# Repacking the pair products of a three-layer CIN kernel: six passes of 128 rows and a shared half pass, operands and weights gathered by row lists

## The chip, the cores and the metric

The kernel runs on one core of one Trainium2 chip, in float32. The metric is the device time of one execution in microseconds. All times quoted are medians of fast runs unless said otherwise. On one core most executions of a kernel agree within about 1%.

## The reference, cut to what matters

```python
B, F, E = (1024, 39, 64)       # batch of x, fields, embedding
HID = [64, 64, 64]

def _cin_layer(Xk, X0, W, b):
    O = W.shape[0]
    Hk, Fdim = (Xk.shape[1], X0.shape[1])
    Wr = W.reshape(O, Hk, Fdim)
    return jnp.einsum('bhe,bfe,ohf->boe', Xk, X0, Wr) + b[None, :, None]

X0 = Xk = sparse_embedding
outs = []
for W, b in ((W0, b0), (W1, b1), (W2, b2)):
    Xk = _cin_layer(Xk, X0, W, b)
    outs.append(Xk.sum(axis=-1))
y = jnp.concatenate(outs, axis=-1) @ fc_w.T + fc_b
```

Both kernels use that only sums over E of the later layers reach the output. The first layer's products x_b * x_a are symmetric, so 39 * 40 / 2 = 780 distinct products a column are enough. A set of weights with 128 columns per chunk of products gives the first layer's 64 outputs and 64 further rows, into which W1, W2 and fc_w were folded beforehand. What remains is one multiplication of the two halves, a sum over E and a small final matmul. "Preparation" below is the folding of the weights and the first fetching of operands.

## The kernel before

The 65536 columns (1024 x 64) are taken in 32 blocks of 2048. The 39 fields lie doubled in DRAM, and four "rolled" copies of 117 = 3 x 39 rows are read from there. A chunk is the elementwise product of two rolls. Six pairs of rolls give 702 products; a seventh chunk, from a roll and a tile q, holds the other 78 and the 39 single fields.

```python
NG = 3
K = NG * F                                   # 117 rows
PAIRS = ((0, 1), (0, 2), (1, 2), (0, 3), (1, 3), (2, 3))
NCHUNK = len(PAIRS) + 1                      # 7

def store(n):
    xd[n] = xds.tile([FW, BLK], F32, name="xd", tag="xd")
    nc.sync.dma_start(xd[n][0:F], xs[n])
    nc.sync.dma_start(xd[n][F:FW], xs[n])

def roll(n):
    r[n] = [rolls.tile([K, BLK], F32, name=f"r{i}", tag=f"r{i}") for i in range(4)]
    for i in range(4):
        nc.sync.dma_start(r[n][i], rows(xd[n], BASE[i], [(1, F), (STEP[i], NG)], BLK))
    qt = q[n % 2]
    nc.sync.dma_start(qt[0:K:NG], xd[n][LAST : LAST + F])
    nc.sync.dma_start(qt[1:K:NG], xd[n][0:F])
# ... preparation: fold W2 (pv, vrow, v2), fold W1 (pt, part), write both doubled to DRAM
#     (wide), gather wa and wb back from there ...
def multiply(n, c, p):
    if c == 0:
        po[n] = [psum.tile([128, SUB], F32, name="po", tag="po") for _ in range(BLK // SUB)]
    for m in range(BLK // MM):
        nc.tensor.matmul(po[n][m // 2][:, bass.ts(m % 2, MM)], wa[:, c, :],
                         p[:, bass.ts(m, MM)], start=(c == 0), stop=(c == NCHUNK - 1))

AHEAD = 4
steps = [(n, c) for n in range(NBLK) for c in range(NCHUNK)]
p = {s: product(*s) for s in steps[:AHEAD]}
for at, (n, c) in enumerate(steps):
    # ... at c == 0: roll(n + 1), store(n + 2), load(n + 3) ...
    if n == 0:
        nc.vector.tensor_tensor(wa[:, c], wa[:, c], wb[:, c], ALU.add)
    multiply(n, c, p.pop((n, c)))
    # ... at c == 0: finish(n - 1), fields(n) ...
    if at + AHEAD < len(steps):
        p[steps[at + AHEAD]] = product(*steps[at + AHEAD])
```

## Time and profile before

| | before |
|---|---|
| time, median of the runs | 862.5 us (861.8 to 863.8) |
| span of the profiled execution (its own time 858.7) | 856.9 us |
| PE busy / DVE busy | 93% / 77% |
| PE without a pause | 97 to 846 us |
| one chunk of 4 matmuls in steady state | 3.442 us |
| lost before PE is full, counted in whole chunks | 76.5 us |
| tail after the last matmul | 9.4 us |

In profiles PE is TensorE, PEld its weight loads, DVE VectorE, ACT ScalarE, POOL GpSimd and SP SyncE; a "q" behind an engine marks the DMAs that it issues.

The profile is read from the outside in. The page says which engine is full and when. The chain of waits says what the end hangs on, and the stretches give each engine's load in the steady part. The timeline then shows what the start waits for. The f32 matmul appears as two records, so one 4-matmul chunk is 8 records. A record's duration includes its latency, so neighbours overlap; the cost of a chunk is read from the spacing, not from the mean.

### The profile page before, as it was taken

What the parts mean: (1) busy time and instruction counts of PE and PEld (TensorE: products, weight loads), DVE (VectorE), ACT (ScalarE), POOL (GpSimd) and SP (SyncE); (2) the same over time, 40 slices, a digit from 0 to 9 for tenths busy, and PEclk for the clock granted to TensorE, in tenths of its full rate; (3) what the DMA queues carried; (4) which work ended last, traced back from release to release, by engine and by line L of the source; (5) the groups of instructions that cost most, each with busy time, mean ns of one, the idle gap of its engine ahead of it and who ended that gap; (6) DMA issues with size and microseconds to landing.
All of it is one profiled execution on the core that took longest, in us unless ns stands there. A gap on an engine that the chain in (4) does not pass through costs nothing.

```text
span 856.9 us, 5040 instructions
## 1 busy us (share of the span) xinstructions
PE 794.1 (93%) x1828; PEld 346.0 (40%) x1828; DVE 664.1 (77%) x372; ACT 140.9 (16%) x133; POOL 44.0 (5%) x54
## 2 busy tenths in 40 slices
PE   1446799999999999999999999999999999999996
PEld 0112344444444444444444444444444444444442
DVE  0333488888888888888888888888888888888883
ACT  0010121122221111122222111122222111112221
POOL 4200000000000000000000000000000000000000
PEclk9998999999999999999999999999999999999998
DMA  6957645767666666665766666755776666565500
GB/s 187 255 142 241 241 177 197 230 210 218 254 240 234 213 233 218 221 215 211 248 242 251 196 237 195 244 215 216 237 242 251 215 225 232 193 210 204 187 0 1
DMA packets 32177, 179.41 MB, mean 209 GB/s; under 512 B 8487, under 2 KB 8686, under 8 KB 11901
## 3 DMA queue, kind: packets, MB, share of 16 engines
q1 hardware_dynamic: 25003, 164.63, 54.9%
q0 software_dynamic: 4080, 11.11, 5.8%
q10 hardware_dynamic: 3070, 3.35, 1.3%
q8 instruction: 14, 0.23, 0.1%
q14 instruction: 10, 0.08, 0.0%
HBM read 156.98 MB, written 23.61 MB: 211 GB/s over the span
## 4 chain that ended last, share of the span: by engine, by line
PE 89%; DMA 7%; issue 1%; DVE 1%; ACTq 1%; SPq 0%; ACT 0%; DVEq 0%
PE po L239 89%; DMA wide<-part 2%; DMA xs<-in_x 2%; DMA r<-xd 1%; DMA v<-vrow 1%; DMA xd<-xs 1%; ACTq L197 1%; DMA wa<-wide 0%; DVE g L262 0%; DVE sums L266 0%; PE pt L186 0%; PE py L295 0%; SPq L200 0%; DVE wa L282 0%; DMA q<-xd 0%
## 5 line engine op out<-in xcount | busy, mean ns | idle before, releaser
L239 PE MATMUL po<-p,wa 117*128 117x512 f32 x1792 | 778.8, 597 | 34.6 <-DVE wa L282 34.6
L232 DVE TENSOR_TENSOR p<-r,r 117x2048 f32<-117x2048 f32 x192 | 436.8, 2289 | 142.9 <-PE po L239 132.3
L239 PEld LDWEIGHTS po<-p,wa 117*128 117x128 f32 x1792 | 342.9, 192 | 469.9 <-issue 422.4
L258 ACT ACTIVATE x<-po,b0s 64x1024 f32<-64x1024 f32 x64 | 71.1, 1112 | 495.7 <-PE po L239 495.7
L251 ACT COPY g<-xs 39x1024 f32<-39x1024 f32 x64 | 66.7, 1043 | 156.4 <-DVE sums L266 156.4
L262 DVE SCALAR_TENSOR_TENSOR g<-po,fc,x 64x1024 f32<-64x1024 f32 x64 | 81.1, 1268 | 9.8 <-ACT x L258 9.8
L266 DVE TENSOR_REDUCE sums<-g 103x16 f32<-103x1024 f32 x64 | 78.1, 1220 | 2.2
L232 DVE TENSOR_TENSOR p<-r,q 117x2048 f32<-117x2048 f32 x32 | 73.1, 2284 | 3.8 <-issue 3.8
L98 POOL DMA_DIRECT2D xs<-in_x x31 | 30.1, 975 | 680.3 <-DMA xd<-xs 397.6
L186 PE MATMUL pt<-w1s,v 64*80 64x512 f32 (+1 forms) x10 | 9.5, 1109 | 13.7 <-DVE v L178 13.7
L222 ACT ACT_TABLE_LOAD x1 | 1.3, 1283 | 57.0 <-DMA wb<-wide 57.0
L186 PEld LDWEIGHTS pt<-w1s,v 64*80 64x80 f32 x10 | 2.2, 228 | 20.4 <-DVE v L178 14.7
L178 DVE COPY v<-v 64x39 f32<-64x39 f32 x1 | 0.2, 176 | 12.9 <-DMA v<-vrow 12.9
L169 PE MATMUL pv<-w2s,fc 64*32 64x312 f32 x16 | 2.5, 724 | 7.9 <-DVE fc L159 7.3
L188 DVE COPY part<-pt 80x512 f32<-80x512 f32 (+1 forms) x5 | 3.4, 673 | 6.8 <-PE pt L186 6.8
L295 PE MATMUL py<-sums,wfin 103*1 103x512 f32 x4 | 2.9, 814 | 3.7 <-DVE sums L266 3.7
L159 DVE COPY fc<-fc 64x32 f32<-64x32 f32 x1 | 0.2, 173 | 6.0 <-DMA fc<-in_fc_w 6.0
L197 POOL DMA_DIRECT2D wa<-wide x6 | 4.1, 686 | 9.5 <-DMA wide<-in_w0t 9.0
L197 POOL DMA_DIRECT2D wb<-wide x6 | 4.3, 716 | 2.2 <-DMA wb<-wide 2.2
L169 PEld LDWEIGHTS pv<-w2s,fc 64*32 64x32 f32 x16 | 0.4, 137 | 9.0 <-DVE fc L159 7.3
L152 POOL MEMSET q<- 117x2048 f32 x2 | 3.6, 1843 | 0.0
L176 DVE COPY vrow<-pv 128x312 f32<-128x312 f32 x2 | 1.0, 482 | 2.7 <-PE pv L169 2.7
(22 smaller groups left out, 9.1 us busy)
## 6 DMA issues: line engine op xcount, KB each, us to landing
r<-xd SPq DMA_DIRECT2D x128, 936.0 KB
xd<-xs SPq DMA_DIRECT2D x64, 312.0 KB
q<-xd SPq DMA_DIRECT2D x64, 312.0 KB
xs<-in_x POOLq DMA_DIRECT2D x31, 312.0 KB, 5.2
wide<-part ACTq DMA_DIRECT2D x8, 160.0 KB
wide<-in_w0t POOLq DMA_DIRECT2D x2, 380.2 KB, 9.7
wide<-in_w0t ACTq DMA_DIRECT2D x2, 380.2 KB
w2s<-in_w SPq DMA_DIRECT2D x1, 624.0 KB
```

Source lines behind the costliest of these rows:

```text
L98: engine.dma_start(xs[n].rearrange("p (b e) -> p b e", e=E), xv[:, n * BB : (n + 1) * BB, :])
L152: nc.gpsimd.memset(qt, 1.0)
L169: nc.tensor.matmul(pv[32 * t : 32 * t + 32, half, 0:n8], fc2, w2s[:, g * n8 : (g + 1) * n8], start=True, stop=True,)
L186: nc.tensor.matmul(pt[0:FX, :n], v2, w1v[:, f0:f1, :], start=True, stop=True)
L188: nc.vector.tensor_copy(part[:, :n], pt[0:FX, :n])
L197: engine.dma_start(dst[:, cols], rows(table, first, steps, H))
L232: nc.vector.tensor_tensor(p, a, b, ALU.mult)
L239: nc.tensor.matmul(po[n][m // 2][:, bass.ts(m % 2, MM)], wa[:, c, :], p[:, bass.ts(m, MM)], start=(c == 0), stop=(c == NCHUNK - 1),)
L251: nc.scalar.copy(gt[H : H + F], xs[n][:, bass.ts(h, SUB)])
L258: nc.scalar.activation(t, po[n][h][H:128, :], AF.Identity, bias=b0s[H:128])
L262: nc.vector.scalar_tensor_tensor(gt[0:H], po[n][h][0:H, :], fc[:, 0:1], x1[h], ALU.add, ALU.mult)
L266: nc.vector.tensor_reduce(sums[:, b_at : b_at + SB], gt.rearrange("p (b e) -> p b e", e=E), AX.X, ALU.add)
```

## The change

The intent was to waste fewer rows of TensorE. Six chunks of 128 rows hold 768 of the 780 products, and what is left over (12 products and 39 single fields) fits into 64 rows, so that two blocks share one pass, each in its own half of the array's rows. The odd row sets can't be described by strides, so operands and weights are fetched by lists of row numbers from tables in DRAM, with indirect DMAs from GpSimd ("gathers"). In the code, r holds the four gathered tiles of a block, u and v are the two factors of a pair's shared half pass, and wa and wb are two gathered sets of weights that VectorE adds once (the "weight add"). The preparation was rebuilt around those tables and its order changed. The core of the diff:

```diff
-NCHUNK = len(PAIRS) + 1
+PAIRS = ((0, 1), (0, 2), (0, 3), (1, 2), (2, 3), (1, 3))
+NPAIR = len(PAIRS)
+NCHUNK = NPAIR + 1
 ...
+    def gather_rows(dst, n, k):
+        table = xd[n // 2 % NTAB][: FT if k < 4 else 2 * FT]
+        nc.gpsimd.indirect_dma_start(
+            dst, None, table, bass.IndirectOffsetOnAxis(ap=lists[:, k : k + 1], axis=0)
+        )
 ...   (lists and wlists: about 60 tiny VectorE instructions from an iota)
+    def weights(c):
+        for k, w in enumerate((wa, wb)):
+            nc.gpsimd.indirect_dma_start(
+                w[:, c], None, table[:], bass.IndirectOffsetOnAxis(ap=wlists[:, k, c : c + 1], axis=0)
+            )
+    weights(0)
+    roll(0, (3,))
+    weights(1)
+    weights(2)
+    roll_half(0)
+    weights(3)
+    roll(1, (0, 1))
+    weights(4)
+    roll(1, (2, 3))
+    weights(5)
+    weights(6)
 ...   (multiply, when c == NPAIR)
+            for h in range(2):
+                w = slice(h * HR, (h + 1) * HR)
+                nc.tensor.matmul(
+                    po[n + h][m // 2][:, at],
+                    wa[w, c, :],
+                    p[w, bass.ts(m, MM)],
+                    start=(h == 1),
+                    stop=(h == 0),
+                )
 ...   (first block)
-        if n == 0:
-            nc.vector.tensor_tensor(wa[:, c], wa[:, c], wb[:, c], ALU.add)
+        if at == 0:
+            for k in range(3):
+                nc.vector.tensor_tensor(wa[:, k], wa[:, k], wb[:, k], ALU.add)
+                if k < 2:
+                    p[steps[2 + k]] = product(*steps[2 + k])
+        elif n == 0 and c + 2 < NCHUNK:
+            nc.vector.tensor_tensor(wa[:, c + 2], wa[:, c + 2], wb[:, c + 2], ALU.add)
```

The small loads of biases moved behind the table's writes, and the last small matmuls (last_weights, with wfin's memset) behind the last block.

## The prediction

> **What bounds the kernel now.** I read the page first (busy shares, slices, costly groups), then the chain in order of time, then the stretches, then the start instruction by instruction. The page, sections 1, 2, 3 and 5:
>
> ```profile
> PE 794.1 (93%) x1828; PEld 346.0 (40%) x1828; DVE 664.1 (77%) x372; ACT 140.9 (16%) x133; POOL 44.0 (5%) x54
> PE   1446799999999999999999999999999999999996
> ...
> q1 hardware_dynamic: 25003, 164.63, 54.9%
> ...
> L239 PE MATMUL po<-p,wa 117*128 117x512 f32 x1792 | 778.8, 597 | 34.6 <-DVE wa L282 34.6
> L232 DVE TENSOR_TENSOR p<-r,r 117x2048 f32<-117x2048 f32 x192 | 436.8, 2289 | 142.9 <-PE po L239 132.3
> ```
>
> PE is full from the sixth slice to the last but one, VectorE (DVE) at eight tenths waits for PE (132.3 us of it), and the only idle time of the main matmul group, 34.6 us, lies at the start. Next the chain in order of time, then the stretches (PE, PEld, DVE, ACT, POOL busy; clock; DMA share; GB/s):
>
> ```profile
> 97.15 748.60 PE po L239 x1740
> 845.83 1.12 ACT x L258
> ```
> ```profile
> 97.00:846.00 749.00, 748.85 (x1741) 331.54 (x1742) 629.99 (x339) 133.78 (x125) 26.11 (x27) 1.00 0.62 213
> ```
>
> From 97 to 846 us PE never pauses, at full clock, while DMA is at 0.62. So a matmul removed there is time gained. A chunk is 8 records (each of the 4 matmuls of 512 columns is two records in f32), so one chunk costs 748.60/(1740/8) = 3.442 us. The kernel has 32 blocks of 7 chunks: 224 x 3.442 = 771.0 us. PE's last chunk ends at about 847.5 us (the tail's second activation starts at 847.55), so 847.5 - 771.0 = **76.5 us are lost at the start**, and 856.9 - 847.5 = 9.4 us are tail. The start, by the timeline:
>
> ```profile
> 15.25 3.04 ACTq L177 DMA_DIRECT2D v<-vrow  x2
> 23.89 0.18 DVE L178 COPY v<-v 64x39 f32<-64x39 f32 x1 [12.87 <-DMA v<-vrow]
> 27.03 15.02 ACTq L190 DMA_DIRECT2D wide<-part  x10
> 46.26 0.87 ACTq L197 DMA_DIRECT2D wa<-wide  x1
> 53.03 6.84 PE L239 MATMUL po<-p,wa 117*128 117x512 f32 x8 [19.04 <-DVE wa L282]
> 59.91 2.29 DVE L232 TENSOR_TENSOR p<-r,r 117x2048 f32<-117x2048 f32 x1 [6.93 <-PE po L239]
> 62.12 0.28 DVE L282 TENSOR_TENSOR wa<-wa,wb 117x128 f32<-117x128 f32 x1
> 62.46 5.40 PE L239 MATMUL po<-p,wa 117*128 117x512 f32 x8 [2.59 <-DVE wa L282]
> ```
>
> Weights pass through DRAM twice (vrow, then part and wide), so the first chunk waits until 53.03. Then block 0 goes in lockstep: a product waits for PE to free its buffer, the weight add stands behind it on DVE, and PE waits for the add: 19.0 us once, then six times about 2.6. Its restarts are slow too (6.84, 5.40 us against 3.442).
>
> **What the Trainium skill says.**
> (1) "TensorE: Matmul & The Clock Gate", Part 3, has matmuls in different row tiles run together, and four K=32 row tiles measured 3.07 times faster. The trace has no row tiles, but it has column tiles in f32:
>
> ```profile
> 7.34 1.27 PE L169 MATMUL pv<-w2s,fc 64*32 64x312 f32 x8 [7.34 <-DVE fc L159]
> ```
>
> Eight records that span 724 ns each (the page) are over in 1.27 us, against 8 x 724 = 5.8 us end to end: they overlap nearly fully. It agrees for columns.
> (2) "TensorEngine Tiling (Array Packing)", Key Properties: changing the mode drains TensorE. No view here prices it.
> (3) "DMA: Bandwidth & Descriptors", the section on why a semaphore goes up by 16: the number of engines is the largest divisor up to 16 of both slowest dims. 117 partitions from 39 rows would give 13 of 16; 128 rows 16. The page's DMA share is a mean over engines and neither confirms nor refutes it.
> (4) "SBUF — State Buffer", SBUF: two separate sides: GpSimd and DVE share a port pair, and descriptors of GpSimd's DMAs can be held up by certain DVE instructions. The trace cannot show it yet: only 5.8% of engine time is on that queue.
>
> **The change part by part.**
> *Chunks.* Before, a block pair takes 14 chunks. After, it takes 12 full ones and one pass that holds both blocks' remainder in rows 0-63 and 64-127: 8 matmuls of 64 rows, in two row tiles and into different banks. The record count stays at 12 x 8 + 16 = 112 a pair, 1792 in all, so only overlap gains. With full overlap the pass costs one chunk, 3.44, plus my estimate of 0.5 us for two drains and a staggered start: 3.94. Pair: 12 x 3.442 + 3.94 = 45.24 against 48.19. Sixteen pairs: 723.8 against 771.0, **-47.2 us**. More rows in a matmul cost nothing: its time goes by the 512 columns.
> *DVE.* 13 products a pair instead of 14: 13 x 2.29 + 4 x (1.27 + 1.22) = 39.7 of 45.2 us, 88%; before 42.0 of 48.2. It stays beside PE.
> *DMA.* A block now gathers 4 MiB for r and half of 2 x 1 MiB for u and v, 5.24 MB, and loads 0.32 MB DRAM to DRAM: 5.56 MB per 22.6 us = 246 GB/s. Before it was 4 x 0.958 + 5 x 0.319 = 5.43 MB per 24.1 us = 225. Per engine: 164.63 MB/(0.549 x 16 x 856.9 us) = 21.9 GB/s, so 16 engines could do some 350. Estimated share about 0.75: hidden if the software queue is as good. r is double, so the next block's gathers have well over a block (about 30 us) between the last read of the old tile and the first product. Five indirect gathers a block at 1 to 2 us of GpSimd each (plain DMAs there take 0.6 to 1.0 us) are at most 10 of 22.6 us.
> *Start.* Estimates from the same operations before. Row lists: some 40 tiny DVE instructions of about 0.1 us, 4 to 5 us, while w2 and x load; lists at 7, x in the table at 8 to 9, three r gathers landed by 20. pv needs one round instead of two: vrow at 11, v2 by 17 (its DMA took 7.8 us before, under traffic). Five pt matmuls now sit two by two in column tiles and their copies are shared with ScalarE: last part at 24.5 instead of 34. Five table writes instead of ten, on two queues: table at 32 instead of 45. Two gathers of 128 rows give chunk 0 its weights: first matmul at about 38 instead of 53. Chunk 0 cold, to 44.5. Then the add is two chunks ahead, so the six waits of 2.6 us and the slow restarts go; but the later weights stand in GpSimd's queue behind 1 MiB gathers (r3, u, v, r of block 1: 7 MiB at 250 to 340 GB/s), so chunks 3 to 5 arrive late by some 7 to 10 us together. I put the end of block 0's seven chunks at 69.6 us: lost 69.6 - 7 x 3.442 = **45.5 against 76.5, -31 us**.
> *Tail.* last_weights moves behind the last block and wfin's memset behind the last reduce on DVE, so both py matmuls wait for it: about +1 us on 9.4.
> Sum: 45.5 + 723.8 + 10.4 = 779.7 us of span. Runs are 862.5 - 856.9 = 5.6 us above the span: 785.3, rounded to **786 us**.
>
> **The rivals.**
> (a) *The row tiles don't overlap.* The pass costs 16 records x 0.43 = 6.9 us, PE gains nothing in the steady part, and only the start counts: 16 x (6.9 - 3.9) = 48 more, 834 us. For it: no row-tiled f32 record in this trace. Against it: the overlap of pv. 13%.
> (b) *The software queue becomes the bound.* If gathers by row lists move below 246 GB/s, say 200, a block takes 5.56/0.2 = 27.8 us and the kernel 900; at 230, 24.2 us and some 840. For it: that queue is barely used now, DVE could hold up descriptors, and its 256-byte writes ran at 11.11 MB/(0.058 x 16 x 856.9) = 14 GB/s an engine. Against it: rows of 8 KB and all 16 engines. 8%.
> (c) *The start gains little*, because one gather queue serializes weights and operands: lost 60 instead of 45.5, 800 us. 20%. Or the traffic is faster than I think: 38, 778 us.
> (d) *DVE becomes the bound*: 39.7 us a pair leaves 5.5; it needs waits of over 0.4 us a product. 4%.
>
> **Range and chances.** The middle is the sum. Down: start at 36 and drains free give about 768. Up: start at 60 plus a half overlap of the pass (+24) gives 824. Rival (a) alone is at 834 and still over 2% faster (845 is the line); only (b) or (d) can reach it. Faster 0.95, within 2% 0.03, slower 0.02.
>
> **What would show it.** In the profile after: a form of 64 x 512 matmuls, 256 records, the pass taking about 3.9 us between full chunks (6.9 if (a)); full chunks still 3.44; PE without waits after block 0 (waits of DVE for r gathers every block if (b)); DVE near 88%; DMA near 0.75 and 246 GB/s; the first main matmul near 38 us and the end of block 0 near 70; a tail of 10 to 11 us. I am wrong if row tiles take turns, if gathers land over 30 us after they are asked for, or if table writes of 256 bytes are far slower than the old ones of 2 KB.

## The result, and the profile after

The kernel after takes 777.5 us (777.1 to 780.9, 4 runs) against 862.3 us for the kernel before in the same rounds. The ratio is 0.902, with a 95% interval of 0.8995 to 0.905. A ratio here is the mean time of one kernel's fast runs over that of the other's fast runs of the same rounds, so it is not quite the ratio of the medians. The profiled execution (777.1 us) has a span of 775.1 us.

The page of the kernel after: busy shares, PE in 40 slices, the gather queue, and the groups that answer to those shown of before:

```profile
PE 735.6 (95%) x1820; PEld 316.8 (41%) x1820; DVE 633.2 (82%) x409; ACT 142.2 (18%) x136; POOL 279.2 (36%) x185
...
PE   3279999999999999999999999999999999999996
...
q0 software_dynamic: 23840, 169.46, 56.0%
...
L341 PE MATMUL po<-p,wa 128*128 128x512 f32 x1536 | 667.8, 596 | 19.3 <-DVE wa L409 15.1
L324 DVE TENSOR_TENSOR p<-r 128x2048 f32<-128x2048 f32 x192 | 435.9, 2291 | 96.9 <-PE po L341 68.3
...
L117 POOL DMA_INDIRECT r<-xd,lists x128 | 211.3, 1651 | 410.5 <-DVE p L324 384.0
...
L352 PE MATMUL po<-p,wa 64*128 64x512 f32 x256 | 59.3, 602 | 0.0
```

PE is now full from the fourth slice. The bulk of the bytes moved from the hardware queue to GpSimd's software queue (q0). There is a new group of 256 matmul records of 64 rows, and its 59.3 us of busy time for records that would take 256 x 0.43 = 110 us in a row says at once that they overlap.

The chain in order of time (start, length, what) gives the price of a pass, and one stretch of a block pair in the steady part gives the load of each engine, in the order of columns told in the prediction:

```profile
63.71 3.63 PE po L352 x16
67.34 41.40 PE po L341 x96
```
```profile
350.00:395.30 45.30, 45.30 (x114) 19.81 (x113) 39.12 (x22) 8.62 (x8) 16.38 (x11) 1.00 0.65 246
```

A half pass costs 3.63 us and twelve full chunks 41.40 us, so a pair costs 45.03 us where it cost 14 x 3.442 = 48.19 us. PE still has no pause, DVE works 39.12 of 45.30 us (86%), and DMA moves 246 GB/s at a share of 0.65.

The start, by the timeline (start, length, engine, line, what, and what ended the idle time before):

```profile
7.75 1.32 SPq L246 DMA_DIRECT2D v<-vrow  x2
...
13.87 5.61 PE L273 MATMUL pt<-w1s,v 64*40 64x512 f32 x10 [6.70 <-DMA v<-vrow]
...
27.41 0.95 POOL L298 DMA_INDIRECT wa<-table,wlists  x1 [11.24 <-DMA bias<-in_b]
...
33.32 5.45 PE L341 MATMUL po<-p,wa 128*128 128x512 f32 x8 [13.84 <-DVE wa L409]
...
53.90 0.29 DVE L413 TENSOR_TENSOR wa<-wa,wb 128x128 f32<-128x128 f32 x1 [5.33 <-DMA wb<-table,wlists]
...
54.24 5.24 PE L341 MATMUL po<-p,wa 128*128 128x512 f32 x8 [3.68 <-DVE wa L413]
...
63.64 3.70 PE L352 MATMUL po<-p,wa 64*128 64x512 f32 x16
```

The first main matmul starts at 33.32 us where it started at 53.03. Later weights are late, though: at 53.90 DVE has waited 5.33 us for the weights of chunk 4, PE therefore 3.68 us, and its restart is slow (5.24 us; from 54.0 to 57.4 us the granted clock is 0.50). Block 0 ends at 67.3 us.

Put together in spans, with PE's last chunk ending at 847.5 us before and 763.7 us after:

| part | before | after | gain |
|---|---|---|---|
| sixteen block pairs | 771.0 | 16 x 45.03 = 720.5 | 50.5 |
| lost at the start (end of PE less the line above) | 76.5 | 43.2 | 33.3 |
| tail (span less end of PE) | 9.4 | 11.4 | -2.0 |
| span | 856.9 | 775.1 | 81.8 |

### The profile page after: what moved, and what is told of

Read it like the earlier page. It is cut to its first block, busy times and chain, and to the rows that moved or that the text cites. A ratio compares the mean times of both kernels' runs of the same rounds, so it can differ in the third digit from the quotient of the medians.

```text
span 775.1 us, 4926 instructions
## 1 busy us (share of the span) xinstructions
PE 735.6 (95%) x1820; PEld 316.8 (41%) x1820; DVE 633.2 (82%) x409; ACT 142.2 (18%) x136; POOL 279.2 (36%) x185
## 3 DMA queue, kind: packets, MB, share of 16 engines
q0 software_dynamic: 23840, 169.46, 56.0%
## 4 chain that ended last, share of the span: by engine, by line
PE 92%; DMA 3%; POOL 2%; DVE 2%; issue 1%; ACT 0%; SPq 0%; POOLq 0%; DVEq 0%; ACTq 0%
PE po L341 83%; PE po L352 8%; DMA r<-xd,lists 1%; DMA table<-part 1%; POOL wa L298 1%; DMA v<-vrow 1%; DMA wb<-table,wlists 1%; POOL r L117 1%; PE pt L273 1%; PE py L427 0%; POOL wb L298 0%; DVE g L376 0%; DVE sums L380 0%; DMA bias<-in_b 0%; DVE fields_of L196 0%
## 5 line engine op out<-in xcount | busy, mean ns | idle before, releaser
L341 PE MATMUL po<-p,wa 128*128 128x512 f32 x1536 | 667.8, 596 | 19.3 <-DVE wa L409 15.1
L324 DVE TENSOR_TENSOR p<-r 128x2048 f32<-128x2048 f32 x192 | 435.9, 2291 | 96.9 <-PE po L341 68.3
L341 PEld LDWEIGHTS po<-p,wa 128*128 128x128 f32 x1536 | 291.5, 191 | 395.3 <-issue 383.6
L117 POOL DMA_INDIRECT r<-xd,lists x128 | 211.3, 1651 | 410.5 <-DVE p L324 384.0
L365 ACT COPY g<-u 39x1024 f32<-39x1024 f32 x64 | 66.6, 1043 | 180.7 <-DVE sums L380 157.2
L352 PE MATMUL po<-p,wa 64*128 64x512 f32 x256 | 59.3, 602 | 0.0
L352 PEld LDWEIGHTS po<-p,wa 64*128 64x128 f32 x256 | 23.4, 186 | 34.7 <-issue 34.7
L326 DVE TENSOR_TENSOR p<-u,v 128x2048 f32<-128x2048 f32 x16 | 36.5, 2284 | 0.0
L117 POOL DMA_INDIRECT u<-xd,lists x16 | 28.4, 1772 | 4.9 <-issue 4.9
L117 POOL DMA_INDIRECT v<-xd,lists x16 | 15.0, 940 | 4.9 <-issue 4.6
(62 smaller groups left out, 21.9 us busy)
```

What stands on the lines that cost most here:

```text
L117: nc.gpsimd.indirect_dma_start(dst, None, table, bass.IndirectOffsetOnAxis(ap=lists[:, k : k + 1], axis=0))
L324: nc.vector.tensor_tensor(p, r[n][:, i], r[n][:, k], ALU.mult)
L326: nc.vector.tensor_tensor(p, ut[n // 2 % 2], vt[n // 2 % 2], ALU.mult)
L341: nc.tensor.matmul(po[n][m // 2][:, at], wa[:, c, :], p[:, bass.ts(m, MM)], start=(c == 0 and first), stop=(c == NPAIR - 1 and not first),)
L352: nc.tensor.matmul(po[n + h][m // 2][:, at], wa[w, c, :], p[w, bass.ts(m, MM)], start=(h == 1), stop=(h == 0),)
L365: nc.scalar.copy(gt[H : H + F], ut[n // 2 % 2][h : h + F, bass.ts(m, SUB)])
```

## The experiments

Twelve kernels ran, and all gave right results. Ratios are to the kernel before in the same rounds, which took 856.0 to 863.5 us in all of them. In the diffs, "-" is the kernel after unless another is named.

### The row tiles one behind the other

```diff
-        for m in range(BLK // MM):
-            for h in range(2):
+        for h in range(2):
+            for m in range(BLK // MM):
                 w = slice(h * HR, (h + 1) * HR)
                 nc.tensor.matmul(po[n + h][m // 2][:, at], wa[w, c, :], ...)
```

> The half pass with its loops exchanged: all four column groups of rows 0-63 first, then all four of rows 64-127. Same 16 records, same work, results right. Theory (two row tiles run together only where records of different tiles are neighbours in the stream, because TensorE starts matmuls in order): the pass costs 16 x 0.43 = 6.9 us instead of 3.63, so 777.5 + 16 x 3.27 = 830 us, and PE stays busy without waits. Rival (TensorE looks far enough ahead to pair the tiles itself): pass 3.6 us, 777 us.

It measured 807.59 us (805.7 to 808.2), ratio 0.940: between the two expectations. A line of the chain in order of time, then weight loads (PEld) of one such pass by the timeline:

```profile
63.60 5.46 PE po L351 x16
```
```profile
440.17 1.16 PEld L351 LDWEIGHTS po<-p,wa 64*128 64x128 f32 x7 [0.24 <-issue]
```

The pass takes 5.46 us, and 16 x (5.46 - 3.63) = 29.3 us is nearly the whole loss (807.6 - 777.5 = 30.1). Both theories were wrong. If a matmul could not begin before those ahead of it in the stream have begun, only the first tile's last record and the second tile's first could run together, and the pass would take 15 x 0.43 = 6.45 us or more. If TensorE paired the tiles by itself, it would be 3.6. This pass began at 438.35; seven weight loads fall within 1.16 us from 440.17 on. So the second tile's stream starts there, when the first tile is at its fifth record of eight. The starts of single records in the kept trace show the same: the first tile's fifth starts 1.821 us into the pass, the second tile's first at 1.827 us, ahead of three records of the first tile (2.250, 2.679 and 3.109 us) that stand before it in the stream. Eight records from 440.2 on at 0.43 us end at 443.6, and the next full chunk began at 443.80.

### The row tiles in groups of four records

```diff
+        for k in range(4 if c == NPAIR else 0):
+            h = k % 2
+            for m in (k // 2 * 2, k // 2 * 2 + 1):
```

> The half pass in groups of four records: two column groups of rows 0-63, two of rows 64-127, and the same again. The run with the tiles in turn took 5.46 us a pass and its weight loads show the second tile starting when the first is at its fifth of eight records. Theory (TensorE looks about four matmul records past the running one and starts one on a free row tile): the second tile's first record is the fourth behind, so the tiles are at most one record of 0.43 us apart: 3.6 to 4.1 us a pass, 777 to 786 us. Rival (two streams of 8 merely overlap by chance of the drain): about 5.4 us a pass, 806 us.

From the chain in order of time:

```profile
63.92 3.74 PE po L352 x16
```

It measured 778.99 us, and 3.74 us a pass: 0.11 more than with finest interleaving. This was the theory's forecast for a reach of about four records. So interleaving in groups of four records costs nearly nothing, and in groups of eight it costs 1.8 us of the possible 3.2. How far the reach goes exactly, and what sets it, stays open.

### No row tiles at all

```diff
+                    for h in range(2):   # once, when the weights of the last chunk are added
+                        w = slice(h * HR, (h + 1) * HR)
+                        nc.vector.tensor_copy(wz[w, h], wa[w, NPAIR])   # the rest of wz is zero
 ...
-                    wa[w, c, :],
-                    p[w, bass.ts(m, MM)],
+                    wz[:, h, :],
+                    p[:, bass.ts(m, MM)],
```

> The remainder as two passes over all 128 rows, with weights that are zero in the other block's half: no row tiles, no change of mode, results right. This is what seven chunks a block cost with the new preparation. Theory: 8 more records of 0.43 us a pair, pass 6.9 us, 777.5 + 16 x (6.9 - 3.63) = 830 us; so of the 84.7 us gained some 52 belong to the row tiles and some 33 to the preparation. Rival (a change of mode or row tiles cost more than the pass shows): below 825 us.

It measured 826.05 us (825.9 to 826.2), ratio 0.961. From the chain in order of time:

```profile
64.70 6.87 PE po L352 x16
71.57 41.20 PE po L342 x96
```

The two passes cost 6.87 us against 3.63, so running two row tiles of 64 rows together is worth a factor of 1.89. Of the 84.7 us gained, some 48.5 hang on the row tiles (826.05 - 777.5; by the traces 16 x (48.07 - 45.03) = 48.6). The expected 52 was 3.5 too many, and the second line says why: without row tiles the full chunks beside the pass are a little faster, 41.20 instead of 41.40 us for twelve. Thirteen chunks at 41.20 / 12 = 3.433 would be 44.63 us, and a pair with row tiles takes 45.03. So entering and leaving the tiled mode costs 0.40 us a pair. The record starts of the kernel after put 0.20 us of it at each border: the two steps around the first record of the pass, and those around the first record behind it, take 1.06 us instead of 0.86.

### The old kernel with only the weight adds moved

```diff
 (kernel before)
-    p = {s: product(*s) for s in steps[:AHEAD]}
+    p = {s: product(*s) for s in steps[:2]}
-        if n == 0:
-            nc.vector.tensor_tensor(wa[:, c], wa[:, c], wb[:, c], ALU.add)
+        (the add two chunks ahead, as in the diff of the change)
```

> The kernel before with one change: in the first block the weights of a chunk are added two chunks ahead, as after the change, and two products instead of four are made before. Theory (the lockstep of product, add and matmul costs six waits of 2.6 us and the slow restarts): chunk 0 at 53, cold, then one chunk every 3.5 us, block 0 ends at about 81 instead of 100.6 us: 862.3 - 20 = 842 us. Rival (the wait is only handed on, to the second block's operands or to weights that land late): 852 us or more.

It measured 837.52 us (836.9 to 840.6), ratio 0.976, 4.5 us better than expected. (The record calls it "unclear" because the interval, 0.971 to 0.981, reaches across the 2% line; it lies clear of 1.) From the chain in order of time:

```profile
53.40 770.92 PE po L239 x1788
```

From its first main matmul on, PE never stops. The first matmul is no sooner (53.40 against 53.03), yet the span falls by 856.9 - 835.1 = 21.8 us. So about two thirds of the 33.3 us that the change gains at the start can be had by this one edit of the old kernel. The other third needs the new preparation, whose own first block is not free of waits.

### Products cut in two, to shorten GpSimd's holds

```diff
-            nc.vector.tensor_tensor(p, r[n][:, i], r[n][:, k], ALU.mult)
+            for s in range(2):
+                cut = slice(s * SUB, (s + 1) * SUB)
+                nc.vector.tensor_tensor(p[:, cut], r[n][:, i, cut], r[n][:, k, cut], ALU.mult)
```

What it tests, in the kernel after by GpSimd's timeline and VectorE's timeline:

```profile
100.02 2.75 POOL L117 DMA_INDIRECT r<-xd,lists  x1 [11.77 <-DVE p L324]
...
105.32 0.94 POOL L117 DMA_INDIRECT r<-xd,lists  x1 [0.30 <-issue]
```
```profile
99.67 2.28 DVE L326 TENSOR_TENSOR p<-u,v 128x2048 f32<-128x2048 f32 x1
101.91 2.29 DVE L324 TENSOR_TENSOR p<-r 128x2048 f32<-128x2048 f32 x1
...
105.34 2.30 DVE L324 TENSOR_TENSOR p<-r 128x2048 f32<-128x2048 f32 x1 [1.14 <-PE po L341]
```

A gather that starts while a product runs ends about 0.8 us after that product's end: the first one above ends at 102.77, and the product of u and v ended at 101.95, although the next followed at once. From 75 us on the kept trace has 72 such gathers, and all end 0.81 to 0.82 us after one product's end. A gather that starts 0.02 us ahead of a product takes its plain 0.94 us, and the product isn't slowed (2.30 against 2.29).

> The kernel after with every product cut into two instructions of 1024 columns. Theory (a gather of GpSimd that starts while VectorE multiplies two SBUF tiles is held until that instruction ends, then takes its 0.94 us): the holds halve, so the mean of the r gathers falls from 1651 to about 1300 ns and the longest from 2.95 to about 2.1 us; the time stays within 1% of 777.5 us, as GpSimd has slack and VectorE loses at most 13 x 0.1 us of its 5 us a pair. Rival (GpSimd's long gathers come from full rings or from DMA traffic): mean stays near 1650 ns.

The time was 776.42 us (775.1 to 776.9), ratio 0.903, within 1% as expected. But the mean of the r gathers rose, from 1651 to 2191 ns. By GpSimd's and VectorE's timelines of this run:

```profile
100.23 5.09 POOL L117 DMA_INDIRECT r<-xd,lists  x1 [10.01 <-DVE p L326]
105.62 1.77 POOL L117 DMA_INDIRECT r<-xd,lists  x1 [0.30 <-issue]
```
```profile
102.15 2.35 DVE L326 TENSOR_TENSOR p<-r 128x1024 f32<-128x1024 f32 x2
105.35 2.36 DVE L326 TENSOR_TENSOR p<-r 128x1024 f32<-128x1024 f32 x2 [0.85 <-PE po L347]
```

The first gather was held until 105.32, past four product instructions in a row, and was let go about 0.8 us after VectorE's first pause (at 104.50). The second ended at 107.39, 0.8 us after the end of the first half of a product (106.58), while the other half ran on to 107.71: this one was let go at the joint, as the theory says. From 75 us on the kept trace has 29 gathers of the first kind, always the first r gather of a block, and 57 of the second. So "until that instruction ends" is refuted as a rule, and the 29 raised the mean: the other 99 r gathers of the run average 1344 ns and take 1.94 us at most, near the forecast. The rival falls as well, for the DMA traffic is the same and only VectorE's instructions differ. What is shown is that the pattern of VectorE's products sets the hold. Why the first gather of a block isn't let go at a joint between two instructions of 1024 columns, where the later ones are, stays open. In the steady part it costs nothing: GpSimd has slack.

### Weights first in GpSimd's queue

```diff
     weights(0)
     roll(0, (3,))
-    weights(1) ... (mixed with roll_half(0) and roll(1))
+    for c in range(1, NCHUNK):
+        weights(c)
+    roll_half(0)
+    roll(1)
```

> The kernel after with GpSimd's queue at the start in another order: all weights before u, v and the second block's r. Theory (chunks 4 and 5 of block 0 wait because their weights stand behind 1 MiB gathers in one queue): those waits, 3.7 us and more, go, but u, v and the next r come some 10 us later and the wait moves to the second block's first product; block 0's waits fall, the end of block 0 moves by 0 to 4 us: 774 to 778 us. Rival (the weights themselves are slow, not their place): the waits for weights stay and the time rises.

It measured 782.15 us (780.8 to 783.3), ratio 0.911: 4.6 us worse than the kernel after, a miss. (The kernel after did not run in these rounds, but the traces agree: block 0 ends at 71.2 us instead of 67.3.) By the timeline:

```profile
59.79 2.29 DVE L321 TENSOR_TENSOR p<-u,v 128x2048 f32<-128x2048 f32 x1 [12.91 <-DMA v<-xd,lists]
...
62.34 5.26 PE L336 MATMUL po<-p,wa 128*128 128x512 f32 x8 [8.62 <-DVE wa L408]
```

The wait before chunk 4 did go (counted from 0). But v landed later, and the product of u and v stands in VectorE's queue ahead of the weight add of chunk 5, so PE waited 8.62 us for an add whose own weights had been asked for by 45.40, before v (51.55). The wait moved not to the second block, as I expected, but to block 0's own half product.

### Operands before the weights' table is complete

```diff
-        roll(0, (0, 1, 2))
+        roll(0)
+        roll_half(0)
 ...   (and the second block's load moved to the front)
```

> The kernel after with the fourth r gather and u and v of block 0 issued before the weights' table is complete, in the 11 us in which GpSimd waits, and with the second block's load moved to the front. Theory (the start is bound by GpSimd's one queue, 24 gathers of 1.25 us and holds after the table is ready): chunk 0 starts within 2 us of 33.3, no later chunk waits more than 2 us, block 0 ends near 60 instead of 67.3 us: 770 us. Rival (3 MiB more ahead in the DMA rings delay the first weights by as much as is gained, or the first loads come later): first chunk after 37 us, 776 us or more.

It measured 783.18 us as the median of its three fast runs, ratio 0.911: the rival's side. (A fourth run took 2794.59 us. The comparison of fast runs leaves it out, and nothing here explains it; with it the median is 784.03.) By the timeline:

```profile
33.00 2.10 ACTq L292 DMA_DIRECT2D bias<-in_b  x2
...
42.09 16.57 PE L340 MATMUL po<-p,wa 128*128 128x512 f32 x32 [22.16 <-DVE wa L408]
```

The bias load, which follows the table's writes in the chain of waits, comes at 33.00 instead of 24.62 us, and the first chunk at 42.09 instead of 33.32. In the chain in order of time the stretch of those writes is 15.81 us long, where it was 6.89, and by the semaphores in the kept traces the last write lands at 35.65 us instead of 26.56. The three gathers of 1 MiB issued into GpSimd's idle time share the DMA engines (a share of 0.93 from 25 to 36 us) with the small table writes that everything waits for. So GpSimd's idle 11 us was not free. The second load moved to the front is part of this run and was not tried alone; it brings 0.3 MB into that time, the gathers 3.1 MB, and with it the folding of W1 began only 0.5 us later (14.33) and the first gather 1.0 us later (13.57).

### Two and four more gathers a block

```diff
                 roll(n + 1)
+                for k in range(2):        # 4 in the second kernel
+                    gather_rows(spare[(n * 2 + k) % 3], n + 1, (n + 1) % 2 * 4 + k)
```

> The kernel after with two more gathers of 1 MiB a block into tiles that nobody reads: 7.7 MB a block instead of 5.56. In 22.5 us that is 340 GB/s. Theory (the gather queue moves 24.4 GB/s on each of 16 engines when busy, so some 390): hidden, DMA share near 0.9, 777 to 785 us. Rival (its ceiling is near the 334 GB/s that the fullest slice shows): some 23 to 24 us a block, 800 to 830 us.

> As the last, with four more: 9.75 MB a block, 433 GB/s in 22.5 us. Both theories have it bound by DMA; it measures the ceiling: at 390 GB/s 25.0 us a block, 855 us; at 335 GB/s 29.1 us a block, 985 us. VectorE should then wait for r gathers in every block.

They measured 777.35 us (ratio 0.905) and 789.78 us (787.1 to 790.2, ratio 0.919). One stretch of 200 us, first with two and then with four more gathers; the last three columns are the clock, the DMA share and GB/s:

```profile
100.00:300.00 200.00, 200.00 (x503) 87.03 (x502) 171.59 (x94) 37.72 (x35) 108.96 (x64) 1.00 0.89 347
```
```profile
100.00:300.00 200.00, 200.00 (x503) 86.94 (x502) 171.56 (x93) 37.70 (x35) 162.34 (x81) 1.00 1.02 421
```

35% more bytes (244.3 MB in all against 181.4) are hidden wholly. With 69% more (307.2 MB), DMA is full at some 420 GB/s. Even so, VectorE waits for r gathers in nearly every block only from 375 us on, and PE for products only from 495 us on; from there a pair takes 46.4 us instead of 45.03, and the loss is 12 us in all. My ceilings of 390 and 335 GB/s were both too low. The kernel after, at 241 to 254 GB/s, has wide room.

### Small loads early

```diff
-        (ones into the other tables, biases, b0, fc_b: behind the table's writes)
+        (the same lines directly after the writes of zeros, in ScalarE's idle time)
```

> The kernel after with the four small loads of biases and the two writes of ones moved from behind the table's writes to ScalarE's idle time at 4 us. Theory (the first weight gather waits for the bias load, 1.9 us behind the last table write, by a shared queue or semaphore): GpSimd's first weight gather starts at 25.5 instead of 27.4 us and block 0 ends 1 to 2 us sooner: 775.5 to 776.5 us. Rival (the table's last write is what it waits for, and the bias load only lands beside it): gather still at 27.4, 777.5 us.

It measured 778.40 us (777.5 to 781.6), ratio 0.903, against 777.75 for the kernel after in the same call. By the timeline:

```profile
28.00 0.95 POOL L298 DMA_INDIRECT wa<-table,wlists  x1 [11.73 <-DVE p L324]
```

The first weight gather starts at 28.00, no sooner. So the releaser that the profile of the kernel after names there, the bias load, is not the cause. With that load gone it names a product of VectorE, which writes nothing that the gather needs. The semaphores in the kept traces name what it waits for, as the rival had it: the last of the five writes of the table (issued at 20.16 us in both). In the kernel after its last share landed at 26.56 us, and GpSimd passed its wait for it at 26.58; in this run the times are 27.02 and 27.05. The gather starts 0.8 to 1.0 us later.

### Four edits at the start, and the kernel after again

```diff
+        nc.vector.memset(wfin[0:H], 1.0)           # at the start instead of behind the last block
+        (small loads early, as above)
     weights(3)
-    roll(1, (0, 1))
     weights(4)
-    roll(1, (2, 3))
     weights(5)
+    roll(1, (0, 1))
     weights(6)
+    roll(1, (2, 3))
-            for k in range(3):                     # adds three chunks ahead instead of two
+            for k in range(4):
```

> Four small edits to the kernel after: small loads early, the weights of chunks 4 and 5 ahead of the second block's first operands in GpSimd's queue (u and v stay where they are, unlike in the run with all weights first), weight adds three chunks ahead instead of two, and the memset of wfin at the start. Theory: no chunk of block 0 waits over 2 us for weights, block 0 ends near 62.5 instead of 67.3 us, the first py matmul runs beside the last reduce: 771 us, 0.8% under the kernel after in the same rounds. Rival (GpSimd's queue after the table is the bound whatever the order): 775 us or more.

> The kernel after itself, unchanged, on the same chip as the three others, to compare with: 777.5 us, first weight gather at 27.4 us, end of block 0 at 67.3 us.

They measured 772.79 us (771.0 to 774.8, ratio 0.897, interval 0.8945 to 0.8997) and 777.75 us (777.5 to 778.9, ratio 0.903, interval 0.9008 to 0.9054). The intervals don't meet, so this version is the fastest of all, by 0.6%. By the timeline:

```profile
59.53 3.70 PE L353 MATMUL po<-p,wa 64*128 64x512 f32 x16 [2.29 <-DVE wa L413]
```

Block 0 ends at 63.2 us instead of 67.3 (62.5 expected), with one wait of 2.29 us before the half pass (none over 2 us expected). Of the 4.1 us, about one is given back in the second block, where PE pauses once for a product (0.96 us) whose r gathers come later now. In spans: the lost start falls from 43.2 to 40.3 us and the tail from 11.4 to 9.7. The four edits were not run one by one, save the small loads, which by themselves gained nothing.

## Why the prediction was right, point by point

The direction, the size and the range held: 786 us predicted, 777.5 measured, range 768 to 824.

- **Chunks.** Right, by the step on which over half of the gain hung: the row tiles overlap. Full chunks cost 3.450 us (3.442 assumed), the pass 3.63 (3.94 estimated), a pair 45.03 (45.24). Of my 0.5 us for drains and a staggered start, 0.2 were measured in the pass itself, and the run without row tiles puts the whole price of the mode at 0.40 us a pair. Rival (a) is refuted by the first profile; the run without row tiles then gave what it would have cost, 826 us, near its 834. One reading on the way was too generous: 8 x 724 ns counts each record's latency. By spacing (0.52 us from the first four pv records to the next four) eight in a row would need some 4.2 us; four of them start 6 to 7 ns apart, so the conclusion holds.
- **DVE.** Beside PE at 86% (88% forecast). Rival (d) did not come.
- **DMA.** 246 GB/s was exact; the share was 0.65 instead of 0.75, because the gathers move 169.46 MB / (0.560 x 16 x 775.1 us) = 24.4 GB/s an engine, not 21.9. Rival (b) is out by far, as the extra gathers show. My third point from the skill, 13 of 16 engines for the old rolls, agrees with the kept traces, though no view prints it: each of the 128 old r loads raises its semaphore 14 times, once early and 13 times as its data lands, and each gather 16 times.
- **Start.** 43.2 us lost instead of 45.5; rival (c), with 60 or 38, did not come. The path was the forecast one, but faster: first matmul at 33.3 instead of 38, as v2 was there at 13.8 instead of 17. Late weights and operands held chunks of block 0, by 1.23, 3.68 and 0.53 us before chunks 1, 4 and 5, with a slow restart of 1.8 us (5.24 less 3.45) on top, 7.2 in all. That this lies in the forecast 7 to 10 is luck: I had chunks 3 to 5 late and no slow restart, and of that 4.2 us came. Nor do my terms give my 69.6: 44.5 + 6 x 3.442 = 65.2, and 7 to 10 more is 72 to 75. So the closeness of 45.5 to 43.2 is in part luck too: the first matmul came 4.7 us sooner than forecast, and block 0 from there took 34.0 us instead of 31.6. Of the things I held responsible for this gain, the end of the lockstep, done alone in the old kernel, gave 21.8 us.
- **Tail.** 2.0 us longer, 1 forecast: both final matmuls waited for the memset behind the last reduce. The last version took it back.
- **A mis-sized term.** "Runs are 862.5 - 856.9 = 5.6 us above the span" set a median against the span of another, faster execution. The profiled execution of before itself took 858.69 us, 1.8 above its span, and after it is 2.0. That accounts for 3.6 of the 8.5 us by which I was too high. The rest is 3.3 at the pairs, 2.3 at the start, -1.0 at the tail, and rounding.

## What to carry to other kernels

When a remainder fills no more than half of the rows, pair it with another remainder in two row tiles, and interleave their matmuls in the stream at least every few records: the same sixteen records cost 3.6 us interleaved, 5.5 in two runs of eight, and 6.9 without row tiles. Before rebuilding a preparation, look for an engine queue in which a small instruction that others wait for (a weight add) stands behind one that waits itself (a product): moving it gave the old kernel 22 us in one edit, and a new order of gathers made the same fault again. An idle issuing engine is no licence to issue early: three MiB of operands asked for in GpSimd's idle time came with small writes on the critical path that landed 9 us later, and the whole lost more than it gained.

## What the Trainium skill lacked or had wrong

- "TensorE: Matmul & The Clock Gate", Part 3, calls matmuls strictly first-in, first-out in start and end. Across row tiles that doesn't fit: with eight records of one tile and then eight of the other, the second tile's first record started 6 ns after the first tile's fifth, and the pass took 5.46 us where starts in order need 6.45 or more. Its factor for row tiles is for four of 32 rows; two of 64 rows in f32 gave 6.87 / 3.63 = 1.89.
- "TensorEngine Tiling (Array Packing)", Key Properties, says that a change of mode drains TensorE and gives no price: here 0.40 us for in and out.
- "DMA: Bandwidth & Descriptors", Bandwidth, says in one place that HBM binds HBM to SBUF traffic at some 358 GB/s, and in its table has 425 GB/s for a large transfer with one core at work. This kernel uses one core, and its gathers of 8 KB rows on the software queue moved 412 to 421 GB/s over stretches of 200 us: the table's figure is the one to plan with here.
- "SBUF — State Buffer", SBUF: two separate sides, has the shared port pair held for a whole instruction, and the loser blocked, in either direction; for VectorE instructions with two SBUF operands it says so only against GpSimd instructions that read SBUF, and reports that such products did not stall DMAs in its own probe. Here they held the issue of gathers, which read their row lists from SBUF: 72 of 72 that started during a product, and one kind for 5.09 us across four instructions of 1.2 us. But a product that started 0.02 us behind a gather was not held (2.30 against 2.29 us).
- No page that I found prices the issue of an indirect DMA on GpSimd: 0.94 us for 128 rows when not held, and 0.30 us until the next.
